# A four-stage conv/Mamba network on one core: tile waits by bytes instead of by pool, and a first Mamba front of its own

## The chip, the cores and the metric

The kernel runs on one core of a Trainium2 chip, as one program from the input image to the output. The metric is the device time of one execution in microseconds (us), smaller being better. Three runs of the kernel before took 8290.22, 8294.99 and 8299.15 us; the median, 8294.99, is what a changed kernel is compared with.

A core has five engines that run side by side and each take their instructions in order: TensorE (PE) multiplies matrices, VectorE (DVE) and GpSimd (POOL) do elementwise work, ScalarE (ACT) applies functions, and SyncE (SP) issues transfers. Semaphores order them.

## The reference

The input x has 4 images of 96 channels and 64 x 64 pixels in float32. Four blocks follow one another, each with weights of its own:

1. A Mamba fusion block. Each image is a sequence of 4096 tokens with 96 features. Two Mamba layers are added to it in turn, and then their output is joined with a pooled vector of the image by a 1x1 product, normalised by a batch norm over all images, and added to the block's input. One Mamba layer is, cut to what matters:

```python
h = layernorm(seq) * ln_g + ln_b
xs, z = split(h @ in_w)                       # 192 channels each
xc = silu(causal_conv(xs, 4 taps) + conv_b)
dt, Bm, Cm = split(xc @ xproj_w)              # 6, 16 and 16 rows
delta = softplus(dt @ dt_w + dt_b)
dA = exp(delta[..., None] * A)
dBx = delta[..., None] * Bm[:, :, None, :] * xc[..., None]
state = scan(dA, dBx)                         # s_t = dA_t * s_(t-1) + dBx_t
y = (einsum('blds,bls->bld', state, Cm) + Dp * xc) * silu(z)
seq = seq + y @ out_w
```

2. An SSD block: a Mamba-2 layer run over each image in four scan directions, with an RMS norm ahead, 3 heads of 64 channels and a state of 128.
3. A second Mamba fusion block.
4. A ConvNeXt block: depthwise convolution, layer norm, two products with a GELU between them, a scale, and the residual.

The batch norm between blocks 1 and 2, and between 3 and 4, needs the mean and the variance of the whole fused output. Nothing of block 2 that depends on normalised values can begin before the last pixel of block 1 is there.

## The kernel before, in words

`program` calls, twice, `mamba_fusion` and then a block: `ssd` the first time and `convnext` the second. A Mamba stage writes its fused output without the batch norm into a DRAM tensor `raw`, and returns two vectors per channel, `bn` (L712 to L724); the block behind it loads `raw` and applies them (for SSD the steps `affine` L871 and `residual` L872, for ConvNeXt L1577 and L1579).

**A Mamba stage.** It takes 32 steps: 4 images, 2 layers, 4 pieces of 1024 tokens. A step is a front and 24 groups.

- The front (`mamba_front`) works on a piece X: `pc` centers it by a matmul (L166), `sq` squares, `pv` averages (L175), `rs` is the inverse root, `h` the normalised input (L182, L185). `pu` multiplies h with the convolution already folded into the input weights (L196, 8 matmuls for each of three channel groups j), `x` is its Silu, `pz`/`z` the gate, `pd`/`dbl` the small projection (L227, L231), which goes to DRAM as `rows` (L235). From there B and C are loaded, spread over partitions, as `bc` (L277). `pt`/`delta` is the softplus (L246), `du` delta times x on POOL (L258); both are stored as `dd` and `dg` (L263).
- A group (class `Scan`) takes 8 of the 192 channels with their 16 states, on 128 partitions, over the two halves of the piece (512 tokens each). It loads `da` from `dd`, and in 7 of 24 groups `du` from `dg` as well (L332, two transfers of 256 KB each, five groups ahead, into 9 buffers). ACT makes the exponential with `w_a` in place (L110). `bs` is du times B: in 17 groups PE spreads it with the selector `seldu` (L346) and DVE multiplies it with bc (L369), in 7 POOL makes the product (L354). DVE scans (L374), POOL multiplies the states `hs` with C into `hc` (L381), PE sums over states with `selsum` (L395), and once per j DVE closes y (L412).
- Behind the last j, PE projects (L425), ACT adds into X (L617), and for layer 2 the piece goes out to `raw` (L632) with sums for the batch norm (L629).

The order of all this is written out by hand in `Scan.run`: for every group it issues the stages with their lags, and inside the groups it advances the front of the next step by a table `PACE` (age of the front in groups, number of parts). Each engine is held to the order in which the code issues. The first front has no groups to run beside: before, it is the same generator `mamba_front`, exhausted before `Scan.run` begins.

**Around the stages** the order isn't written by hand. The set-up of a stage (weights, constants made by memsets and selects, first loads) stands in the code behind the stage ahead, and the scheduler of the tile framework may put an instruction earlier on its engine when what it depends on allows that. That is where the pools come in. All tiles come from tile pools, two to four for each stage (`m1`, `mwork`, `mstate`; `s1`, `swork`; `c1`, `cwork`; and one in PSUM each). Pools of a stage are closed at its end and their bytes given to the next stage's pools. By the framework's default a tile of a new pool waits for every user of the pool that had its bytes before:

```python
one = ctx.enter_context(tc.tile_pool(name="m1", bufs=1))
work = ctx.enter_context(tc.tile_pool(name="mwork", bufs=1))
psum = ctx.enter_context(tc.tile_pool(name="mps", bufs=2, space=PSUM))
```

The tiles at the boundaries that later sections name are, in SSD: `ones`, `tri`, `mask` (a triangle of ones), `inw` and `conv` (the input weights, and convolution weights multiplied by them, L805, from which `sconv` is spread), `xn` (the normed input with its border, memset at L785), the pieces `X` of `raw`, `pk` (packed input for the matmuls) and `dr`. In Mamba: `one`, `seldu`, `selsum`, the weights `w_...`. In ConvNeXt: `band` (four padded images, memset at L1563, filled at L1579), `quad`, `taps`, `diag` (the depthwise weights as diagonals, L1597 to L1606), `shifted` and `strips` (copies of the band for PE and DVE, L1623, L1625), `dw` and `acc` (the convolution on PE and on DVE, L1661, L1676).

Of the kernel before, what the change touches and what calls it, by code (L numbers as in the profile page):

```python
# [18 lines left out]
F32 = mybir.dt.float32  # L19
# [106 lines left out]
def rsqrt(act, out, in_, eps):  # L126

    act.exp_ln(out, in_, AF.Ln, bias=eps)
    act.exp_ln(out, out, AF.Exp, scale=-0.5)


# [15 lines left out]
def mamba_front(tc, k, x_in, pools, wt, parts, c, h, made):  # L147
# [148 lines left out]

PACE = {
    0: 2, 1: 1, 2: 1, 3: 1, 4: 1, 6: 1, 7: 2, 8: 1, 9: 2, 10: 1, 11: 2, 12: 1, 13: 2, 15: 1, 16: 1,  # L300
    17: 2, 18: 1, 19: 1, 20: 1, 21: 1, 22: 1, 23: 1, 28: 1, 29: 1, 30: 1, 31: 1,
}
# [5 lines left out]
class Scan:  # L308
# [125 lines left out]
    def run(self, steps, wts, front, first, later):  # L434
# [18 lines left out]
        for n in range(-LEAD, total + 26):  # L453
# [28 lines left out]
            for began, parts in fronts:  # L482
                for _ in range(PACE.get(n - began, 0)):
                    next(parts, None)
# [76 lines left out]
def mamba_fusion(ctx: ExitStack, tc, k, src, dst, w):  # L561

    nc = tc.nc
    one = ctx.enter_context(tc.tile_pool(name="m1", bufs=1))

# [14 lines left out]
    fetch(2)  # L580
    work = ctx.enter_context(tc.tile_pool(name="mwork", bufs=1))
    state = ctx.enter_context(tc.tile_pool(name="mstate", bufs=3))
    psum = ctx.enter_context(tc.tile_pool(name="mps", bufs=2, space=PSUM))
    dram = ctx.enter_context(tc.tile_pool(name="mdram", bufs=3, space=DRAM))
# [17 lines left out]
    for b in range(2):  # L602
# [3 lines left out]
        )  # L606
    for q in range(NQU):
        pq = psum.tile([P, T], F32, tag="mm", name="pq")[:, :QUART]
        nc.tensor.transpose(pq, sel["du"][:QUART, 0, q], k.ident[:QUART, :QUART])
        nc.vector.tensor_copy(sel["sum"][:, q], pq)  # L610

# [34 lines left out]
    def front(n, made):  # L646
        b, sub, c = steps[n]
        pooled = None if sub else parts[:, b]
        return mamba_front(
            tc, k, chunks[b * NS + c], (work, psum, dram), wts[sub], pooled, c, h, made  # L650
        )

    for _ in range(4):
        fetch()
# [4 lines left out]
    gpw = one.tile([C, C], F32, name="gpw")  # L659
    made = {}  # L660
    for _ in front(0, made):
        pass

    def other_weights():

        yield from mamba_weights(nc, k.act, k.ident, one, w, 1, wts[1])
        nc.sync.dma_start(gpw, w["gp_wT"])
        nc.sync.dma_start(fus, w["fus_wT"].rearrange("(q c) o -> c q o", q=2))
        nc.sync.dma_start(vec, w["vecs"])
        yield  # L670
# [14 lines left out]
    def pooled_rows(b):  # L685
# [13 lines left out]
    each = 3 * HALFP // HEIGHT  # L699
    later = [(each, other_weights()), (2 * each - 2, folded())] + [  # L700
        ((2 * b * NS + NS) * each - 2, pooled_rows(b)) for b in range(B)
# [44 lines left out]
class Ssd:  # L746
# [7 lines left out]
    def __init__(self, ctx, tc, k, src, dst, w):  # L754
        nc = self.nc = tc.nc
        self.k, self.w, self.dst = k, w, dst
        self.raw, self.res, self.bn, self.src = src
        one = self.one = ctx.enter_context(tc.tile_pool(name="s1", bufs=1))
        self.work = ctx.enter_context(tc.tile_pool(name="swork", bufs=2))
        self.psum = ctx.enter_context(tc.tile_pool(name="sps", bufs=2, space=PSUM))  # L760
        self.dram = ctx.enter_context(tc.tile_pool(name="sdram", bufs=2, space=DRAM))
# [32 lines left out]
    def weights_of(self, w):  # L794
# [4 lines left out]

        conv = self.work.tile([P, 3 * BLK], F32, tag="pk", name="conv")  # L800
        conv = conv[:C, : 4 * DI].rearrange("c (k n) -> c k n", k=4)
        nc.sync.dma_start(conv, w["conv_wT"][:, :DI].partition_broadcast(C))
# [742 lines left out]
def convnext(ctx: ExitStack, tc, k, src, out, w):  # L1545

    raw, before, (bn_scale, bn_shift), src = src
    nc = tc.nc
    one = ctx.enter_context(tc.tile_pool(name="c1", bufs=1))
    work = ctx.enter_context(tc.tile_pool(name="cwork", bufs=2))  # L1550
    psum = ctx.enter_context(tc.tile_pool(name="cps", bufs=2, space=PSUM))

# [136 lines left out]
    def bank(tag, bufs):  # L1689
        return psum.tile([P, T], F32, tag=tag, name=tag, bufs=bufs)  # L1690
# [193 lines left out]
```

## Time and profile before

| | us |
|---|---|
| Median of three runs (8290.22 to 8299.15) | 8294.99 |
| The profiled execution: own time | 8294.08 |
| The profiled execution: span | 8292.4 |
| Mamba 0 (to its bn vector) | 0 to 2703 |
| SSD (to its last x store) | 2703 to 4997 |
| Mamba 1 | 4997 to 7707 |
| ConvNeXt | 7707 to 8292 |
| First scan of Mamba 0 / of Mamba 1 | 66.8 / 5060.1 |
| DVE, POOL, PE, ACT busy, of the span | 91%, 82%, 87%, 63% |

The span is the time between the first and the last instruction that the profiler recorded; the own time is what the same execution took by the device's clock, 1.7 us more. A stage has no mark of its own in the trace. Its borders are read from instructions: the end of `bn`, the last store of x. The busy shares are averages over four stages with different limits, so they say little on what a stage waits for. Windows cut at the borders say more.

In a line of the timeline the columns are start, duration, engine (SPq is SyncE's queue of transfers), line of the code, operation, output and inputs, shapes and count, and in square brackets the idle time of the engine before it and what ended that. A row of the waits is: engine, what waited, what it waited for, total us, times, and the longest.

### The profile page before, as it was taken

Reading aid. Unit: us, or ns where it says so; the run is one execution under the profiler, and the core shown is the slowest. Engines: PE = TensorE matmul, PEld = TensorE weight load, DVE = VectorE, ACT = ScalarE, POOL = GpSimd, SP = SyncE. Lnnn points to the kernel's source line nnn. Section 1 sums busy time; section 2 is a strip of 40 time slices with the busy share of each in tenths; the row PEclk is TensorE's granted clock in tenths of the full one; section 3 lists DMA queues with packets and bytes.
Section 4 is the critical chain, followed back from the end, with each engine's and each line's share of the span. In section 5 each row is a group of like instructions: output and inputs, shape, how many; then the busy total and the mean of one; then the engine's idle time right before and its main releaser. Section 6 shows DMA issues by size and latency. Waiting matters only on the chain. (4 is left out here: it accounts for less than half of the span.)

```text
span 8292.4 us, 111766 instructions
## 1 busy us (share of the span) xinstructions
PE 7184.2 (87%) x33944; PEld 3173.3 (38%) x33944; DVE 7523.9 (91%) x8897; ACT 5227.7 (63%) x9510; POOL 6788.3 (82%) x4589
## 2 busy tenths in 40 slices
PE   7888888888887899999999997888888888887688
PEld 1222222222221687898888882222222222221122
DVE  6999999999998799998999996999999999999786
ACT  5666666666664677777777765666566666655255
POOL 6999999999998587887878886999999999999211
PEclk9999989999998899999999998999999999988799
DMA  7989889999997433433333326999898999888553
GB/s 195 240 234 250 232 238 242 238 238 246 246 233 198 116 94 105 113 100 115 96 109 109 93 77 179 240 239 248 230 244 239 245 236 247 236 231 223 120 128 75
DMA packets 819139, 1558.50 MB, mean 188 GB/s; under 512 B 117613, under 2 KB 123529, under 8 KB 815466
## 3 DMA queue, kind: packets, MB, share of 16 engines
q1 hardware_dynamic: 815466, 1546.23, 71.0%
q8 instruction: 272, 4.46, 0.2%
q10 hardware_dynamic: 3072, 5.11, 0.2%
q14 instruction: 329, 2.70, 0.1%
HBM read 1256.10 MB, written 148.50 MB: 169 GB/s over the span
## 5 line engine op out<-in xcount | busy, mean ns | idle before, releaser
L381 POOL TENSOR_TENSOR hc<-hs,bc 128x1024 f32<-128x1024 f32 x1536 | 3603.4, 2361 | 404.1 <-DVE hs L374 314.1
L374 DVE TENSOR_TENSOR_SCAN hs<-da,carry,bs 128x1024 f32<-128x1024 f32 x816 | 1914.9, 2347 | 121.6 <-issue 47.0
L346 PE MATMUL bs<-du,seldu 64*128 64x512 f32 x4352 | 1420.8, 696 | 652.7 <-DVE hs L374 647.4
L369 DVE TENSOR_TENSOR bs<-bs,bc 128x1024 f32<-128x1024 f32 x1088 | 1319.7, 1213 | 113.4 <-PE bs L346 91.4
L110 ACT ACTIVATE da<-da,w_a 128x1024 f32<-128x1024 f32 x1088 | 1230.7, 1140 | 5.3 <-DMA da<-dd 3.1
L354 POOL TENSOR_TENSOR du<-du,bc 128x1024 f32<-128x1024 f32 x448 | 1060.0, 2366 | 26.5 <-DMA da<-dd 13.7
L346 PEld LDWEIGHTS bs<-du,seldu 64*128 64x128 f32 x4352 | 396.8, 199 | 1629.0 <-issue 1160.0
L395 PE MATMUL py<-hc,selsum 128*32 128x512 f32 x6144 | 838.5, 616 | 33.3 <-DVE y L412 20.6
L110 ACT ACTIVATE bs<-da,w_a 128x1024 f32<-128x1024 f32 x448 | 500.2, 1116 | 534.2 <-DVE hs L374 244.4
L196 PE MATMUL pu<-h,w_conv 96*64 96x512 f32 (+1 forms) x3072 | 824.1, 657 | 7.8 <-ACT h L185 7.2
L374 DVE TENSOR_TENSOR_SCAN hs<-bs,carry,du 128x1024 f32<-128x1024 f32 x336 | 781.4, 2326 | 0.0
L374 DVE TENSOR_TENSOR_SCAN hs<-da,bs 128x1024 f32<-128x1024 f32 x272 | 622.1, 2287 | 40.3 <-issue 14.1
L1129 DVE SCALAR_TENSOR_TENSOR bc<-front,taps,bc 128x384 f32<-128x384 f32 (+1 forms) x1152 | 648.8, 564 | 0.5
L1094 PE MATMUL front<-sconv,pk 128*128 128x192 f32 x3072 | 596.3, 331 | 16.9 <-ACT z L1146 11.8
L1254 POOL TENSOR_TENSOR xs<-x,coef 128x576 f32<-128x576 f32 x512 | 590.8, 1154 | 16.4 <-DVE y L1332 14.8
L1323 POOL TENSOR_TENSOR y<-y,xs 128x192 f32<-128x192 f32 x496 | 294.3, 593 | 363.0 <-DVE y L1316 358.7
L1338 ACT ACTIVATE y<-yz 128x192 f32<-128x192 f32 x512 | 183.9, 359 | 548.2 <-DVE yz L1333 475.7
L1223 POOL TENSOR_TENSOR seg<-dr,mask 128x384 f32<-128x384 f32 x512 | 512.3, 1001 | 9.7 <-DMA dr<-rows 9.7
L1094 PEld LDWEIGHTS front<-sconv,pk 128*128 128x128 f32 x3072 | 493.8, 192 | 28.0 <-ACT z L1146 18.6
L110 ACT ACTIVATE seg<-seg,ndac 128x128 f32<-128x128 f32 x1536 | 499.2, 388 | 4.5 <-POOL prev L1282 1.3
L1676 DVE SCALAR_TENSOR_TENSOR acc<-strips,kern,acc 128x512 f32<-128x512 f32 x504 | 425.4, 846 | 51.0 <-ACT acc L1666 18.3
L115 ACT ACT_TABLE_LOAD x352 | 451.6, 1283 | 8.6 <-ACT dtrow L938 3.0
(225 smaller groups left out, 12778.7 us busy)
## 6 DMA issues: line engine op xcount, KB each, us to landing
da<-dd SPq DMA_DIRECT2D x3072, 256.0 KB
du<-dg SPq DMA_DIRECT2D x896, 256.0 KB
dr<-rows SPq DMA_DIRECT2D x256, 384.0 KB
bc<-rows SPq DMA_DIRECT2D x256, 256.0 KB
dd<-delta SPq DMA_DIRECT2D x192, 256.0 KB
dg<-du SPq DMA_DIRECT2D x192, 256.0 KB
pk<-xn SPq DMA_DIRECT2D x128, 384.0 KB
pk<-xn SPq DMA_DIRECT2D x128, 256.0 KB
```

The lines of the kernel that those rows point to most:

```text
L110: self.last = self.scalar.activation(out, in_, func, **kw)
L196: nc.tensor.matmul(pu[HALFP * i : HALFP * (i + 1)], lhsT=wt["conv"][:kk, tap, D0[j] : D0[j] + HALFP], rhs=h[:kk, ds(i * T + tap, T)], star ...
L346: nc.tensor.matmul(g["bs"][:, i], lhsT=self.sel["du"][rows, g["half"], g["q"]], rhs=g["made"]["du"][rows, g["j"]], start=True, stop=True,)
L354: self.tc.nc.gpsimd.tensor_tensor(g["du"], g["du"], self.b_or_c(g, 0), ALU.mult)
L369: nc.vector.tensor_tensor(dbx, dbx, self.b_or_c(g, 0), ALU.mult)
L374: nc.vector.tensor_tensor_scan(out, da, dbx, init, ALU.mult, ALU.add)
L381: nc.gpsimd.tensor_tensor(g["hc"], hs, self.b_or_c(g, 1), ALU.mult)
L395: nc.tensor.matmul(py[ds(HALFP * i + QUART * x["half"], QUART)], lhsT=self.sel["sum"][:, q], rhs=x["hc"][:, i], start=(q == 0), stop=(q == ...
L1094: nc.tensor.matmul(p, lhsT=held["pk"][:, i, ds(order[m] * Q, Q)], rhs=self.conv[:, i], start=(i == 0), stop=(i == 2),)
L1129: nc.vector.scalar_tensor_tensor(out, shifts[tap], self.taps[:, q, tap : tap + 1], out, ALU.mult, ALU.add)
L1223: self.nc.gpsimd.tensor_tensor(seg, g["pair"]["dr"][:, ds(g["c"] % 2 * NH, NH)], self.mask[:, g["r"]].to_broadcast([P, NH, Q]), ALU.add,)
L1254: self.nc.gpsimd.tensor_tensor(xs, x.to_broadcast([P, 3, NH, HD]), coef.to_broadcast([P, 3, NH, HD]), ALU.mult)
```

## The change

The change has three parts.

1. The pools of a stage are taken apart. A class `Laid` opens many small pools with `reuse_waits="tile"`, each for one or a few tags, in a written order; with it a tile waits only for users of the bytes that it takes over. The order lays the tiles of a stage by when the stage ahead is done with those bytes. The PSUM pools are treated likewise, one for each tag. `work`, `state` and `one` become names for the same set of pools.
2. The first front of a Mamba stage is a routine of its own, `first_front`. In it the convolution of group j goes from PSUM through Silu straight into x, and the gates likewise, between them; h is scaled on DVE, not ACT; dbl is evicted by DVE; the two averages `pv` have a PSUM bank each; the copies of X that sum for the pooled vector come at its end. It yields once delta is made, and the rest (the remaining stores, products and bc loads) is issued inside the first groups through `later`, from group -5 on. The transposes that make `selsum` come behind it (`sum_rows`). The front of the second step follows a table `LATE`, which starts at an age of 5 groups and has the same entries as `PACE` from 16 on.
3. SSD's convolution weights get a tile of their own, `convw`, where they were in a slot of `pk`.

The diff, cut to its core:

```diff
+class Laid:
+    def __init__(self, ctx, tc, name, order, **space):
+        self.pools = {}
+        for i, tags in enumerate(order):
+            pool = ctx.enter_context(
+                tc.tile_pool(name=f"{name}{i}", bufs=1, reuse_waits="tile", **space)
+            )
+            self.pools.update(dict.fromkeys(tags.split(), pool))
+
+    def by(self, bufs):
+        return LaidPool(self.pools, bufs)
...
+def first_front(tc, k, x_in, pools, wt, parts, h, made):
...
+    for n, tag in enumerate(("po", "py")):
+        pc = bank("mm", 2)[:C]
+        nc.tensor.matmul(pc, lhsT=k.center, rhs=xs[n], start=True, stop=True)
+        sq = work.tile([P, T], F32, tag="ua", name="sq", bufs=3)[:C]
+        nc.scalar.activation(sq, pc, AF.Square)
+        pv = bank(tag, 1)[:C]
+        nc.tensor.matmul(pv, lhsT=k.mean, rhs=sq, start=True, stop=True)
+        rs = work.tile([P, T], F32, name="rs", bufs=2)[:C]
+        rsqrt(k.act, rs, pv, k.eps[:C])
+        nc.vector.tensor_tensor(into[n], pc, rs, ALU.mult)
+        nc.vector.tensor_scalar(
+            into[n], into[n], wt["ln"][:, 0:1], wt["ln"][:, 1:2], ALU.mult, ALU.add
+        )
...
+    for j in range(3):
+        pu = bank("mm", 2)
...
+        k.act.other(x[:, j], pu, AF.Silu, back=False)
+        if j == 1:
+            gate(0)
+    pd = bank("po", 1)
+    for j in range(3):
+        if j == 2:
+            gate(1)
+        rows_of(pd, j)
+    gate(2)
+    dbl = work.tile([P, T], F32, name="dbl")
+    nc.vector.tensor_scalar_add(dbl, pd, wt["one"])
+    rows = dram.tile([P, T], F32, name="rows")
+    nc.sync.dma_start(rows, dbl)
...
+        k.act.other(deltas[j], pt, AF.Softplus, back=(j == 2))
+        if j == 0:
+            store("dd", 0, deltas[0])
+            spread(0)
+            sized(0)
+    for n in range(2):
+        unused = work.tile([P, T], F32, tag="ua", name="copy", bufs=3)[:C]
+        nc.scalar.activation(unused, xs[n], AF.Copy, accum_out=parts[:, n : n + 1])
+    yield
+    store("dg", 0, du[:, 0])
+    sized(1)
+    yield
...
+LATE = {
+    5: 2, 6: 1, 7: 1, 8: 2, 9: 2, 10: 2, 11: 2, 12: 2, 13: 2, 14: 2, 15: 1, 16: 1,
+    17: 2, 18: 1, 19: 1, 20: 1, 21: 1, 22: 1, 23: 1, 28: 1, 29: 1, 30: 1, 31: 1,
+}
...
-                for _ in range(PACE.get(n - began, 0)):
+                for _ in range((LATE if began < 0 else PACE).get(n - began, 0)):
...
-    one = ctx.enter_context(tc.tile_pool(name="m1", bufs=1))
+    laid = Laid(ctx, tc, "m", (
+        "h w_ln0 w_in0 w_conv0 w_xproj0 w_dt0 w_dd0 w_d0 w_a0 w_out0 one7", "dbl", "delta", "rs",
+        "seldu", "du", "x", "ua", "bc", "X", "z", "hs", "da", "y", "hc", "*",
+    ))
+    one = work = state = laid.by(1)
...
-    psum = ctx.enter_context(tc.tile_pool(name="mps", bufs=2, space=PSUM))
+    psum = Laid(ctx, tc, "mps", ("mm", "po", "py", "bs"), space=PSUM).by(2)
...
+    ahead = first_front(tc, k, chunks[0], (work, psum, dram), wts[0], parts[:, 0], h, made)
+    next(ahead)
+    sum_rows()
...
-    for _ in front(0, made):
-        pass
...
-    later = [(each, other_weights()), (2 * each - 2, folded())] + [
+    later = [(-5, ahead), (each, other_weights()), (2 * each - 2, folded())] + [
...
+        laid = Laid(ctx, tc, "s", (
+            "ones tri norm epsn inw convw sconv xbias bcbias taps a ad", "xn0 xn1", "pk", "nx nr", "nsq",
+            "dtx ua row", "z", "X", "mask opw gn", "*",
+        ))
+        one, self.work = laid.by(1), laid.by(2)
...
+        self.psum = Laid(ctx, tc, "sps", ("front", "halves", "y", "out"), space=PSUM).by(2)
...
-        conv = self.work.tile([P, 3 * BLK], F32, tag="pk", name="conv")
-        conv = conv[:C, : 4 * DI].rearrange("c (k n) -> c k n", k=4)
+        conv = one.tile([C, 4, DI], F32, name="convw")
...
+    laid = Laid(ctx, tc, "c", (
+        "taps kern conv_b quad diag c_vecs c_w1 c_b1 c_w2 shift", "turned", "band0", "band1",
+        "band2", "band3", "raw before", "*",
+    ))
+    one, work = laid.by(1), laid.by(2)
+    psum = Laid(ctx, tc, "cps", ("hid", "dw", "ln", "out"), space=PSUM).by(2)
```

## The prediction

> **What bounds the kernel now.** I read the windows table first, cut where the stages change: Mamba 0 runs to 2703 us, the SSD block to 4997, Mamba 1 to 7707, the ConvNeXt block to the end. Its columns after the window are busy us (instructions) of PE, PEld, DVE, ACT and POOL, then granted TensorE clock, DMA share, GB/s.
>
> ```profile
> 0.00:67.00 67.00, 43.78 (x120) 12.15 (x122) 8.03 (x20) 34.57 (x48) 11.92 (x16) 0.92 0.49 131
> 67.00:148.00 81.00, 65.00 (x260) 15.43 (x256) 77.72 (x46) 52.16 (x81) 73.23 (x33) 0.89 0.96 243
> 148.00:2600.00 2452.00, 2101.11 (x8341) 512.30 (x8341) 2329.56 (x1395) 1549.88 (x2305) 2276.79 (x1022) 0.94 0.92 240
> 2600.00:2677.00 77.00, 54.53 (x182) 13.47 (x182) 71.84 (x43) 25.25 (x31) 66.84 (x30) 0.75 0.63 160
> 2677.00:2703.00 26.00, 17.67 (x24) 4.16 (x24) 4.34 (x12) 4.08 (x12) 3.27 (x2) 0.55 0.07 22
> 2703.00:2797.00 94.00, 68.72 (x232) 38.54 (x233) 48.64 (x106) 47.35 (x89) 20.10 (x19) 0.71 0.47 130
> 4955.00:4992.00 37.00, 26.42 (x181) 21.77 (x179) 24.42 (x61) 14.64 (x58) 28.25 (x38) 1.00 0.00 1
> 4992.00:5060.00 68.00, 42.69 (x118) 15.57 (x120) 7.39 (x16) 33.18 (x47) 11.40 (x10) 0.72 0.56 153
> 7600.00:7681.00 81.00, 54.62 (x192) 13.32 (x190) 75.85 (x45) 28.35 (x34) 70.69 (x31) 0.79 0.62 160
> 7707.00:7741.00 34.00, 9.31 (x72) 2.75 (x76) 14.09 (x19) 4.26 (x6) 9.28 (x4) 0.59 0.65 147
> ```
>
> Inside a Mamba stage DVE is the bound (2330 of 2452 us, 95%), with POOL at 93% and DMA at 92% close behind. Between stages nobody is: DVE works 8 of the first 67 us, 4 of 26 at 2677, 7 of 68 at 4992, 14 of 34 at 7707. Then DVE's waits say what it waits for at the beginning (0 to 67 us) and around 5000:
>
> ```profile
> DVE h L182 <- ACT rs L110: 43.2, 4, 34.0
> DVE h L182 <- ACT rs L110: 36.7, 4, 26.5
> DVE h L594 <- DMA x<-X: 7.8, 1, 7.8
> ```
>
> The timeline shows the last two as a chain, and the same behind the other boundaries:
>
> ```profile
> 4990.88 0.69 DVE L1388 TENSOR_TENSOR X<-X,out 96x256 f32<-96x256 f32 x1 [1.21 <-PE out L1371]
> 4991.60 3.51 SPq L1395 DMA_DIRECT2D x<-X  x4
> 4998.87 0.10 POOL L587 MEMSET one<- 128x1 f32 x1 [12.44 <-DMA x<-X]
> 5037.01 0.34 SPq L235 DMA_DIRECT2D rows<-dbl  x1
> 5046.81 2.45 SPq L332 DMA_DIRECT2D da<-dd  x4
> 5060.13 2.29 DVE L374 TENSOR_TENSOR_SCAN hs<-da,bs 128x1024 f32<-128x1024 f32 x1
> ...
> 2703.30 3.51 POOL L785 MEMSET xn<- 1x4102 f32 x1 [21.74 <-DVE bn L724]
> 2719.53 0.95 DVE L805 TENSOR_TENSOR conv<-conv,inw 96x768 f32<-96x768 f32 x1 [7.18 <-DMA inw<-in_L_in]
> ...
> 7707.40 9.28 POOL L1563 MEMSET band<- 96x2692 f32 x4 [21.74 <-DVE bn L724]
> 7709.79 6.94 DVE L1604 COPY quad<-ident 32x32 f32<-32x32 f32 x3
> ```
>
> The reader is to see that a memset, which needs nothing but its own bytes, waits 12 or 22 us for the last user of the whole former pool; behind it hang all weights, and from there 61 us (4999 to 5060) pass to the first scan.
>
> **The change, by parts.** The instruction counts barely move: over the program DVE gets 6 instructions more (four h multiplications and two dbl evictions that ACT had), ACT 16 fewer, 6 table loads (1.28 each) among them, PE, POOL and the DMA count are unchanged. Inside the stages the waits on the scans, bs products and loads are the same but for a handful. So the 2452-us bodies are costed at nothing, and the sum is made of four boundaries.
>
> *Start (0 to 67).* The new front squares straight away, starts the convolution matmuls with the first h, applies Silu from PSUM group by group (six of about 0.6 us, beside PE), and puts dbl on DVE. Before: h ready at 17.8 and 23.9, convolution to 35.3, then copies, a table load 1.28 and Silu 1.48 over 1536 columns, rows stored at 43.5, delta at 48.1, da loads at 53.8, first scan 66.8. Walking the new order with those durations: h at 16.5, first third of the convolution at about 23 (w_a still lands at 21.6), rows at 35, dd at 38, da loads at 40, first scan about 47, 20 us earlier. But the next 81 us run at a DMA share of 0.96 and 243 GB/s: a 256-KB load costs 256/243 = 1.08 us and a group needs two (four in 7 of 24 groups). In the old order part of that queue was filled while DVE idled; a scan that starts 20 us earlier starts with fewer groups in hand. I give back 7: **13** (8 to 19). The second front is paced to begin later but stores its rows at the same place (group 16), so nothing there: PE, 65 of 81 us busy, has to hide it, and each group that it slips costs 81/24 = 3.4.
>
> *Mamba 0 to SSD (2677 to 2797).* Weights, tri, mask, residual and first X loads go ahead of the batch-norm vector bn (2702.9). What must follow bn are the affine steps. Before, the first ran at 2706.3, the third only at 2720.0, since its loads sat in SP behind others that waited; after that a chunk takes 3.75 us, and the last xn ends at 2745.2. With three X chunks ready at bn and ACT busy about 2.9 us per chunk the eight take 25 to 30 us: last xn near 2730, 15 earlier. Price in the tail of Mamba 0: DVE gets the conv product (0.95, at L805 it waited 7.2 for its load), ones 0.17, memsets 0.6; POOL 1.1 for tri and 3.5 for one xn memset, ahead of the last two hc; SP gets about 1 MB (4 us at 240 GB/s) in a stretch with a DMA share of 0.63. I charge 3: **12** (5 to 17).
>
> *SSD to Mamba 1 (4955 to 5060).* All weights, X loads and selectors go ahead of the four x stores, and the new front interleaves with the last projections: h at 4996.5 where it was 5012.5, rows about 5015.5 (5037.0), da loads 5020.4 (5046.8), first scan 5028 (5060.1), 32 earlier; the same warm-up gives back 6. Price: the SSD tail is paced by POOL (28.3 of 37 us), which gets seldu's memset 0.95, two selects of 2.05 and two of 0.23, 5.5 in all; DVE gets 3 us, ACT the exponential of w_a, which is queued ahead of SSD work and needs all 16 w_a loads (11.6 us of issue). These follow the last dr load on SP, well ahead, in a stretch with DMA at 0.00. Charge 4: **22** (12 to 30).
>
> *Mamba 1 to ConvNeXt (7600 to 7741).* Band memsets, taps, quad and diag go into Mamba 1's tail; the raw loads stay behind the last raw stores. The band additions, which stood behind the quad copies (7716.8 to 7722.3), follow the affines at about 7709 to 7714; first acc at 7734 where it was 7741.1: 7 gained. Against it stand 4 quad and 7 taps copies on a DVE that is 94% busy (75.85 of 81). A taps copy alone takes 0.16, a quad copy beside a POOL memset 2.3 (above: three in 6.94), ending each time with the memset. The Trainium skill, "SBUF — State Buffer", section Who interferes with whom, says why this speaks against the change: a copy that DVE runs over both port pairs and a GpSimd instruction exclude each other for the whole instruction, and whichever begins first blocks the other. By the rule each copy, and diag (0.96, two SBUF inputs), may wait for the rest of an hc (2.36, POOL 87% busy): 12 x 1.18 x 0.87 = 12 us on average, 25 at most. The nearest row of the trace for the other end: the scalar product of w_a at 195.8, in a stretch where POOL is 93% busy, took 0.15, since it stood right behind a scan and hc started after it; 12 such cost 2 to 3. In the new order half of the copies stand behind a scan, half behind a bs product with an hc under way: 8. **-1** (-12 to +8).
>
> Sum 13 + 12 + 22 - 1 = 46. The profiled execution took 8294.1 (its span is 8292.4), 0.9 under the median 8295.0; 8294.1 - 46 = 8248, as a median **8249**.
>
> **The rivals.**
> *A, the warm-up takes it back.* DMA (0.96) and POOL (73 of 81) are as full as DVE just behind both Mamba starts. For it: if the old first scans lived on loads queued during the idle time, 12 to 15 us of each start come back instead of 6 or 7, and the tails cost half as much again as my charges of 3, 4 and 8: 46 - 14 - 7 = 25 gained, 8270. Against: the 24th group comes 80 us after the first scan both in the start and at 5060, hardly slower than the 79 to 85 of a later step.
> *B, the waits stay.* A tile's bytes may have late users (bn's chain, the last hc), or the queue order holds the set-up back; then only the new front gains, perhaps 12: 8283, same. Against: the program's order shows the set-up in front of bn and of the x stores.
> *C, slower: an instruction of the next stage stands at the head of an in-order queue and waits for a transfer.* Place: DVE's conv product ahead of some twenty scans of Mamba 0, behind its own load, which stands in SP behind da loads that wait for buffers that DVE frees; and w_a's exponential in the SSD tail. A wait stops DVE, then the da loads behind the sconv copies on SP. Price: 7.2 us as DVE waited at L805, 11.6 for w_a, and after each a refilling of the 5-group lead, 17 us (5 x 3.4): 24 and 29; with 25 for the copies 78. The four parts gain 61 before my charges (46 + 3 + 4 + 8): 17 slower, 8312. It decides from 61 us of such stalls on. Against: both loads are issued groups ahead.
>
> **How the numbers follow.** Forecast 0.62, A 0.20, B 0.06, C 0.12. About 0.2% (17 us) is what a measurement of this kernel can tell from no change (its runs lie between 8290 and 8299). Faster 0.62 + 0.20 = 0.82, same 0.06, slower 0.12. The four parts' bounds, not all at one end, give 8222 to 8272; the range reaches into B: 8220 to 8283, which leaves out C and the far ends.
>
> **What would show it.** Right: first scan at 45 to 50 us and the 24th group's at 130 to 136 (now 146.0); last xn 25 to 30 us behind bn; first scan of Mamba 1 within 40 us of the last SSD addition (now 69); no POOL memset with 12 or 22 us of idle time before it; quad copies of mixed length, 0.1 to 2.4, among the last scans. Wrong: Mamba bodies whose length changes by over 5 us, a DVE or ACT wait of over 5 us on a weight load before bn or before the last x store, or a first scan early and a 24th group no earlier than now.

## The result, and the profile after

The changed kernel takes 8267.86 us (median of 5 runs, 8253.47 to 8274.96) against 8294.99 us of the kernel before: a ratio of 0.9964 with a 95% interval of 0.9949 to 0.9978. It is faster by 27 us where 46 were forecast. The profiled execution has a span of 8266.1 us. A second set of five runs gave 8272.77 us against 8296.29.

The windows of the profile after, cut at the events themselves where those shown of before are cut near them (columns as there):

```profile
0.00:47.40 47.40, 33.82 (x106) 10.57 (x106) 8.46 (x21) 19.19 (x33) 9.60 (x15) 0.96 0.40 103
47.40:136.50 89.10, 69.99 (x262) 17.65 (x264) 77.65 (x47) 56.09 (x86) 73.67 (x34) 0.83 0.95 259
2589.20:2676.10 86.90, 54.94 (x182) 13.62 (x182) 78.52 (x50) 27.57 (x34) 73.19 (x32) 0.76 0.68 176
2676.10:2701.10 25.00, 18.54 (x24) 4.20 (x24) 4.21 (x19) 4.08 (x12) 7.09 (x3) 0.52 0.35 104
4925.40:4983.00 57.60, 46.80 (x251) 39.59 (x251) 38.36 (x95) 26.68 (x89) 46.10 (x59) 0.76 0.22 54
4983.00:5017.00 34.00, 26.85 (x101) 7.95 (x99) 4.85 (x10) 15.40 (x27) 3.71 (x3) 0.95 0.41 126
5017.00:5106.50 89.50, 70.27 (x262) 17.69 (x264) 77.66 (x47) 56.14 (x86) 73.94 (x34) 0.83 0.95 257
7488.30:7663.00 174.70, 123.67 (x438) 29.97 (x440) 163.63 (x101) 75.47 (x109) 150.18 (x66) 0.80 0.75 191
7689.10:7713.70 24.60, 10.28 (x76) 3.10 (x80) 3.01 (x7) 4.27 (x6) 0.53 (x1) 0.61 0.83 184
```

The idle stretches are shorter, as the change says: 47.4 us to the first scan, 34.0 from SSD's last addition to Mamba 1's first scan, 24.6 from bn to ConvNeXt's first acc. But the rows beside them are longer. For the same work the kernel before shows, in the same view:

```profile
66.80:146.00 79.20, 63.45 (x252) 15.27 (x248) 75.95 (x45) 50.16 (x78) 71.23 (x33) 0.89 0.96 240
4943.50:4991.60 48.10, 35.91 (x244) 29.65 (x243) 34.46 (x88) 24.24 (x83) 39.75 (x53) 1.00 0.06 18
7518.50:7683.20 164.70, 120.66 (x443) 29.12 (x440) 152.26 (x87) 75.49 (x109) 147.10 (x65) 0.84 0.76 201
```

These are the first step of Mamba 0 (79.2, after 89.1), SSD's last ten additions (48.1, after 57.6) and the last two steps of Mamba 1 (164.7, after 174.7). The first step of each Mamba stage went from 79.3 and 79.9 us, first scan to first scan, to 89.2 and 89.5. In Mamba 0's, VectorE stands idle for 11.4 us where it stood for 3.2; the other 1.7 us are more work of VectorE, most of it the second front's h, which stood ahead of the first scan before. In the timeline after, the chain at 4983 reads:

```profile
4982.25 0.72 DVE L1547 TENSOR_TENSOR X<-X,out 96x256 f32<-96x256 f32 x1 [1.90 <-PE out L1530]
4983.00 3.28 SPq L1554 DMA_DIRECT2D x<-X  x4
5005.29 0.34 SPq L391 DMA_DIRECT2D rows<-dbl  x1
5011.25 1.16 SPq L483 DMA_DIRECT2D da<-dd  x2
5017.03 2.29 DVE L525 TENSOR_TENSOR_SCAN hs<-da,bs 128x1024 f32<-128x1024 f32 x1 [1.96 <-ACT da L110]
```

From the last addition's end to rows it is 22 us (before 45), to the da loads 28 (before 55). No memset stands behind the stores any more.

### The profile page after: what moved, and what is told of

Same layout as the page of the kernel before. It is cut to its first block, busy times and chain, and to the rows that moved or that the text cites. A ratio compares the mean times of both kernels' runs of the same rounds, so it can differ in the third digit from the quotient of the medians.

```text
span 8266.1 us, 111696 instructions
## 1 busy us (share of the span) xinstructions
PE 7193.8 (87%) x33944; PEld 3180.7 (38%) x33944; DVE 7532.2 (91%) x8903; ACT 5208.4 (63%) x9494; POOL 6790.8 (82%) x4589
## 5 line engine op out<-in xcount | busy, mean ns | idle before, releaser
L505 POOL TENSOR_TENSOR du<-du,bc 128x1024 f32<-128x1024 f32 x448 | 1060.9, 2368 | 24.4 <-DMA du<-dg 14.4
L546 PE MATMUL py<-hc,selsum 128*32 128x512 f32 x6144 | 840.7, 617 | 37.9 <-DVE y L563 24.5
L220 PE MATMUL pu<-h,w_conv 96*64 96x512 f32 (+1 forms) x2976 | 792.2, 654 | 11.3 <-ACT h L209 11.3
```

The lines of the kernel that those rows point to most:

```text
L220: nc.tensor.matmul(pu[HALFP * i : HALFP * (i + 1)], lhsT=wt["conv"][:kk, tap, D0[j] : D0[j] + HALFP], rhs=h[:kk, ds(i * T + tap, T)], star ...
L505: self.tc.nc.gpsimd.tensor_tensor(g["du"], g["du"], self.b_or_c(g, 0), ALU.mult)
L546: nc.tensor.matmul(py[ds(HALFP * i + QUART * x["half"], QUART)], lhsT=self.sel["sum"][:, q], rhs=x["hc"][:, i], start=(q == 0), stop=(q == ...
```

## The experiments

The places in eight of the profiles, in us, read from scans, additions and bn in each trace: a step or a tail goes from the start of its first instruction to the end of its last (the first step of Mamba 1 to the start of the second), and the stretches between them are what is left. "24th group" is the scan that the prediction calls so, the first of the second step. The medians come from four sets of runs, each with runs of before beside it.

| | before | after | front_alone | pools_alone | mended | pace | less_dma | best |
|---|---|---|---|---|---|---|---|---|
| 0 to the 24th group's scan | 146.0 | 136.5 | 135.0 | 151.2 | 137.8 | 134.9 | 133.4 | 138.4 |
| last step of Mamba 0, scans | 80.9 | 86.9 | 80.8 | 86.8 | 87.4 | 86.8 | 87.5 | 80.8 |
| last scan to last xn of image 0 | 66.1 | 52.8 | 66.2 | 52.8 | 49.2 | 52.8 | 52.8 | 53.0 |
| SSD's last ten additions | 48.1 | 57.5 | 50.2 | 56.9 | 49.6 | 58.7 | 54.8 | 49.4 |
| last addition to first scan | 68.6 | 34.1 | 50.6 | 54.3 | 34.9 | 40.0 | 34.7 | 40.8 |
| first step of Mamba 1 | 79.9 | 89.5 | 86.9 | 79.8 | 86.5 | 79.8 | 86.0 | 83.7 |
| last two steps of Mamba 1, to bn | 188.6 | 200.8 | 187.9 | 197.2 | 188.4 | 199.7 | 201.8 | 193.2 |
| bn to first acc | 34.0 | 24.6 | 33.8 | 24.5 | 27.0 | 24.9 | 25.3 | 27.6 |
| sum, less that of before | 0 | -29.5 | -20.8 | -8.7 | -51.4 | -34.6 | -35.9 | -45.3 |
| median time of the runs | 8295 to 8299 | 8267.9, 8272.8 | 8278.7 | 8268.9, 8269.2 | 8259.2 | 8259.0 | 8253.6 | 8248.9 |

**The front alone** (new `first_front` and `LATE`, pools of before):

```diff
-    laid = Laid(ctx, tc, "m", (...))
-    one = work = state = laid.by(1)
+    one = ctx.enter_context(tc.tile_pool(name="m1", bufs=1))
+    work = ctx.enter_context(tc.tile_pool(name="mwork", bufs=1))
+    state = ctx.enter_context(tc.tile_pool(name="mstate", bufs=3))
...
```

> The new first front with its pacing, in the old pools with their old waits. Theory (the gains are those of separate places, and each start gives back what its warm-up takes): first scan at about 47 us and about 5040 (20 earlier each), the 24th group's scan 9 to 10 us earlier than before in each Mamba stage, the set-up of SSD and ConvNeXt as before, no conv product waiting on VectorE at 2630; in all 18 to 20 us faster than before, 8275. Rival (the front brings something only where the pools let it start early): 9 us, all of it at the first start, 8286.

Measured: 8278.72 us, ratio 0.9976 (0.9966 to 0.9986). First scan at 47.2; in each stage the 24th group gains 10 to 11 us (135.0 for 146.0, and 50.6 + 86.9 for 68.6 + 79.9). The tails are as before. The theory holds; the routine brings 11 us per start, not 20, since the first step takes 88 and 87 us where it took 79 and 80.

**The pools alone** (the opposite half: `Laid` and `convw`, front of before), run twice:

> The laid pools with tile waits and the convw tile, with the old first front. Theory (separate places): the first 24 groups as before; SSD's last first-image xn 14 us sooner after bn; the conv product again stops VectorE for about 6 us in Mamba 0's tail and the quad copies cost about 7 us in Mamba 1's; SSD's tail about 9 us longer; Mamba 1's first scan about 12 us sooner after the last SSD addition. Sum 5 to 12 us faster than before, 8285. Rival (set-up in the tails costs as much as it brings): within 4 us of before, or slower.

> The kernel of pools_alone once more, profiled and timed again. By the places at the boundaries its profile was 9 us shorter than the one before, but its median was 28 us lower; the other 20 us lie in the long Mamba and SSD bodies (groups 96 to 720 of Mamba 1 took 2109 us, before 2126). Theory (the bodies scatter by some 10 us from execution to execution and the pools alone bring about 9): body of Mamba 1 2113 to 2125 in this profile, median 8280 to 8290. Rival (the laid pools make the bodies shorter): body below 2112 again, median about 8269.

Measured: 8268.92 and 8269.17 us, ratios 0.9963 (0.9949 to 0.9978) and 0.9969 (0.9956 to 0.9981). Most places are as expected: set-up of SSD 13 us shorter, conv product waiting 5.1 us, SSD's tail 9 longer, Mamba 1's first scan 14 sooner. One is not: the 24th group of Mamba 0, expected as before, comes 5 us later (151.2 for 146.0) in both profiles, since the first scan comes at 71.0 and 70.9 for 66.8; no run looks into why. The places sum to 9 us, and the median gained 27 to 28. The expectation of 8285 was wrong, in both runs. In the profiles 9 to 13 us of the rest lie where the change has nothing: groups 24 to 720 of Mamba 1 took 2365 and 2369 us with these pools, 2378 in both profiles of before. In the changed kernel, with the same pools, they took 2382 and 2368, so the pools aren't shown to be the cause. Why the same instructions run shorter there was not found out, and with it the medians of the halves (18 and 28 us) don't add up to that of the whole, while their places (20.8 and 8.7) do.

**The kernel before and the changed kernel, profiled again:**

> The kernel before, profiled a second time, for the scatter of what no part of the change touches. Theory (scatter): boundaries the same to within 1 us as in the first profile; the three bodies (2115, 2126 and 2127 us) each within 12 us of the first. Rival (before's bodies are long in every execution): Mamba 1's body again 2124 or more.

> The changed kernel once more, profiled and timed beside the others. Theory (its gain is what the boundaries show, 29 us): first scan 19 us earlier, 24th group 9 to 10 us earlier, conv product waiting 5 to 7 us, SSD's last ten additions 57 us, one quad copy after another beside POOL; median 8262 to 8272. Rival (the gain also lies in the bodies): the three bodies together 15 us or more shorter than before's 6368.

Before took 8287.42 us in this one run. Its boundaries repeat within 1.5 us but for SSD's tail (50.6 for 48.1), and so do its bodies (2112, 2126, 2125; first 2115, 2126, 2127). So the rival of the first expectation came true: Mamba 1's body is not scattered in before, it is 2126 both times. The changed kernel repeats at the boundaries (57.5 for SSD's tail, 174.7 for the last two steps of Mamba 1, the conv product waiting 6.2 us), but for the first steps: 87.1 and 87.2 us where the first profile has 89.2 and 89.5. Its median, 8272.77, is a little above the expected range. Its three bodies sum to 6365 and 6363, before's to 6368 and 6363: in these profiles its gain is at the boundaries.

**The default waits between the small pools:**

```diff
-                tc.tile_pool(name=f"{name}{i}", bufs=1, reuse_waits="tile", **space)
+                tc.tile_pool(name=f"{name}{i}", bufs=1, **space)
```

> The changed kernel with the default waits between pools (a tile waits for all users of the small pools whose bytes its pool takes), layout and front kept. Theory (what counts is that a tile waits only for its own bytes): the set-up of SSD starts behind bn again in large part, and that of Mamba 1 behind the last x store: total 10 to 18 us slower than the changed kernel, 8280. Rival (the order of the small pools does it, the waits by tile add nothing): within 5 us of the changed kernel, 8268, with the same instructions ahead of bn.

Measured: 8266.86 us (0.9963, 0.9949 to 0.9978), the changed kernel's time, with the conv product ahead of bn (it waits 6.0 us at 2638) and 34.1 us from last addition to first scan. The rival holds: taking the large pools apart, in this order, does it. Waits by tile add nothing that these runs can see. What the title and the first part of the change call waits by bytes is, in its effect, the taking apart of the pools. Whether the written order or the bare splitting does it, and how much of it hangs on `convw` (the tile that lets the conv product go ahead), no run separates.

**Mended tails:**

```diff
-        nc.vector.tensor_copy(quad[part, 0], k.ident[part, part])
+        nc.scalar.copy(quad[part, 0], k.ident[part, part])
...
-        nc.sync.dma_start(conv, w["conv_wT"][:, :DI].partition_broadcast(C))
+        nc.scalar.dma_start(conv, w["conv_wT"][:, :DI].partition_broadcast(C))
...
-        nc.gpsimd.memset(x, 0.0)
+        if n < 2:
+            nc.gpsimd.memset(x, 0.0)
+        else:
+            nc.gpsimd.tensor_scalar(x, bn_shift.to_broadcast(x.shape), 0.0, 0.0, ALU.mult, ALU.mult)
...
+        nc.sync.dma_start(
+            sel["du"], k.saved[:, 1:].rearrange("p (b q m) -> p b q m", b=2, q=NQU)
+        )
```

> The changed kernel with four costs of the tails taken away: the conv weights' load is issued by ScalarE instead of behind the da loads, so that the conv product has its data (6.3 us of VectorE idle before); the four quad copies on ScalarE (7 us); the zeroing of bands 2 and 3 made to follow bn (2.1 us); the selector of Mamba 1 loaded from a copy that Mamba 0 saved, not built on POOL (5 us of POOL in SSD's tail). Theory (these costs are what the prediction mis-sized in the tails, each in full): last Mamba 0 step 81 us again, SSD's last ten additions 4 to 5 us quicker, Mamba 1's last two steps 8 to 10 us quicker: 16 to 21 us faster than the changed kernel, 8248. Rival (VectorE's waits only move to the next late thing, a da load or POOL): at most 8 us, 8260.

Measured: 8259.19 us (0.9954, 0.9942 to 0.9966), 9 below the changed kernel where 16 to 21 were expected (22 by the places; in this profile SSD's body was 2133 us for 2125). Two of the four costs went as the theory says, or better. SSD's tail, in the same windows as above, is back:

```profile
4936.80:4986.40 49.60, 39.58 (x251) 33.67 (x251) 38.15 (x95) 26.67 (x89) 40.77 (x53) 0.93 0.30 72
```

POOL has 40.8 us of work for 46.1, and PE's granted clock is 0.93 for 0.76. With the quad copies on ScalarE the last two steps of Mamba 1 take 164.4 us for 174.7, and with the bands zeroed behind bn the stretch from their end to bn takes 23.9 for 26.1, so 188.4 for 200.8 in all. But the bands' zeroing only moved: from bn to the first acc it is 27.0 us for 24.6. The fourth failed: the conv product waited 6.7 us as before, now for inw, whose load I had left on SP.

**inw on ScalarE's queue too:**

```diff
-        nc.sync.dma_start(self.inw, w["in"])
+        nc.scalar.dma_start(self.inw, w["in"])
```

> The mended kernel with inw's load issued by ScalarE as well; in the mended kernel the conv product still waited, for inw. Theory (VectorE stood still for 6 us only because the load was issued just ahead): wait for the load under 1 us, the last Mamba 0 step 81 us instead of 87, total 5 to 6 us below the mended kernel, 8253. Rival (the load isn't served faster than 7 us beside the da loads and VectorE only waits at another place): step still 86 or 87.

Measured: 8254.42 us (0.9948, 0.9936 to 0.9960). The last step is 80.1 us, as the theory says, but the step before is 91.3 for 83.7. The trace names it (the tile's instructions, and what they waited for):

```profile
L979 DVE TENSOR_TENSOR convw<-convw,inw x1: 954/954/954, 2593.6 to 2593.6; 96x768 f32<-96x768 f32 x1
its engine sat idle before it (us, times) until:
  DMA convw<-in_L_conv_wT: 9.8, 1
```

The scheduler put the product earlier along with its load, and the load, issued at 2576.4 among da loads, landed at about 2593. The trace gives 2592.8 for inw, issued at 2574.1. The rival holds: the wait moved, and grew.

**A warm PE** (mended_inw, and two matmuls without use per group at the end of each Mamba stage):

```diff
+            for _ in range(2 if total - 20 <= n < total + 3 else 0):
+                warm = self.psum.tile([P, T], F32, tag="mm", name="warm")
+                self.tc.nc.tensor.matmul(
+                    warm, lhsT=self.k.ident, rhs=made[-1]["x"][:, 0], start=True, stop=True
+                )
```

> The same as mended_inw, with two matmuls whose result nobody reads put on PE per group over the last 20 groups of each Mamba stage and three behind. Last scan to bn took 25 or 26 us with a granted clock of 0.52 and 19.5 with 0.70. Theory (a PE that waits much is granted half the clock, and the last projections then run at 1.06 us each instead of 0.53): granted clock in that stretch 0.9 or more, last scan to bn 17 to 19 us at both boundaries, total 10 to 14 us below mended_inw. Rival (the clock does not follow the filler matmuls, or they delay the bs products by as much): within 4 us of mended_inw or slower.

Measured: 8257.12 us (0.9950, 0.9937 to 0.9962). The clock follows, the time doesn't. From last scan to bn of Mamba 0, with the clock at 1.00, and in pools_alone without the filler:

```profile
2706.60:2727.20 20.60, 15.85 (x47) 4.80 (x45) 9.09 (x24) 4.08 (x12) 9.45 (x3) 1.00 0.49 143
```

```profile
2684.00:2703.50 19.50, 13.09 (x24) 2.99 (x24) 4.16 (x19) 4.08 (x12) 6.97 (x3) 0.71 0.44 132
```

The rival holds, in its second half. Last scan to bn is 20.6 and 22.5 us where mended_inw has 18.7 and 25.2 (granted clock 1.00 and 0.82 for 0.79 and 0.50), and the last xn follows 27.7 us later for 33.5; but the last step takes 90.1 and 87.7 us for 80.1 and 81.6. In Mamba 0's, VectorE waits 6.8 us for bs products from PE where it waited 1.0, and 2.8 for a set-up tile of SSD. (A last projection of Mamba 0 takes 1.06 us in the changed kernel, as the expectation says, and 0.59 here, not 0.53.) The stretch to bn alone misleads, too: in the kernels with laid pools it is 19 us with 33.5 to the last xn behind it, or 25 with 27.8, and the sum is 52.3 to 53.1 in all but mended (49.2) and warm (48.3).

**The pacing, and lighter first loads.** These two look into the first step:

```diff
-                for _ in range((LATE if began < 0 else PACE).get(n - began, 0)):
+                for _ in range(PACE.get(n - began, 0)):
```

> The changed kernel with the second front of each stage paced by the old table (it starts with the loop, not 5 groups later). Theory (the first 24 groups run 10 us long because the first loads come late and ScalarE and TensorE pass that on: h of the second front stands behind an exponential that waits for a da load, the conv matmuls behind h, a bs product behind those): with h and the conv matmuls ahead of the first group, the 4.5-us wait for PE in group 3 goes, the first scan comes 3 to 8 us later, and the 24th group's scan within 3 us of the changed kernel's; total the same, 8268. Rival (the pacing is what costs the start): the 24th group's scan 5 us or more earlier in both stages, total 8258.

```diff
-                last=(q == NQU - 1 and p == 1), dma=(p == 1 and (q % 2 == 0 or (j, q) == (2, 1))),
+                last=(q == NQU - 1 and p == 1),
+                dma=(p == 1 and (q % 2 == 0 or (j, q) == (2, 1))) and (n, j) != (0, 0),
```

> The changed kernel with the two groups of j = 0 in every step 0 (the very first step of the program only for the pair: image 0, layer 1, piece 0 of each Mamba stage) that load du made from PE and VectorE instead: 1 MB less to load in the first 12 groups, two POOL products less, two VectorE products of 1.21 us more. Theory (DMA bandwidth and POOL's late product set the warm-up): the waits of VectorE for POOL's du (2.5 and 3.3 us) and about half of the wait for PE vanish; the 24th group's scan 2 to 5 us earlier after the first scan, in each stage. Rival (the order on ScalarE and PE sets it): VectorE's 2.4 us of more work appear in full, 24th group 0 to 3 us later.

Measured: pace 8258.99 us (0.9950, 0.9936 to 0.9965), less_dma 8253.61 (0.9948, 0.9936 to 0.9959). With pace the first scan is at 54.2, 7 later, and the first step takes 80.7 and 79.8: the 24th group comes 1.6 us earlier in Mamba 0 and 3.8 in Mamba 1 (0.4 and 2.5 against the second profile of the changed kernel). By the places that is the theory with an edge for the old table: what the new pacing wins ahead of the first scan it pays behind it. The total is the one that the rival forecast, 8258, but from 8238.86 to 8273.44 its six runs cover the theory's 8268 too, so the total decides nothing. For less_dma, VectorE's waits in the first groups of the changed kernel and of this one are

```profile
DVE bs L520 <- PE bs L497: 4.8, 2, 4.5
DVE hs L525 <- POOL du L505: 2.5, 1, 2.5
DVE hs L525 <- ACT da L110: 2.1, 1, 2.1
```

```profile
DVE hs L525 <- ACT da L110: 1.3, 1, 1.3
DVE h L206 <- ACT rs L110: 1.2, 1, 1.2
```

Two groups whose du need not be loaded take away the waits for POOL and for PE, and the 24th group comes 3 us earlier in both stages (1.8 and 1.5 against the second profile of the changed kernel), with 2.4 us more of VectorE's work. That is the theory's side, but the edit takes POOL's two products out along with the loads, so the loads alone aren't shown to set the warm-up, and the first step still takes 84.3 and 86.0 us where before has 79.3 and 79.9. The total moved by more than the places (36 us by places, 46 by medians).

**All together:**

```diff
-        nc.vector.tensor_tensor(conv, conv, xs[:, None].to_broadcast([C, 4, DI]), ALU.mult)
+        unit = one.tile([C, 1], F32, name="unit")
+        nc.vector.tensor_scalar(unit, self.bn[1], 0.0, 1.0, ALU.mult, ALU.add)
+        nc.vector.scalar_tensor_tensor(
+            conv, conv, unit, xs[:, None].to_broadcast([C, 4, DI]), ALU.mult, ALU.mult
+        )
...
```

> Everything that the runs point to in one kernel: the changed kernel, with the quad copies on ScalarE, bands 2 and 3 zeroed behind bn, Mamba 1's selector loaded from a copy, the sign of a turned on ScalarE, the two first du loads replaced as in less_dma, the old pacing of the second front, and the conv product made to follow bn (multiplied by a one that is computed from bn). Theory (each cost was in one place): no VectorE wait for a conv load, last Mamba 0 step 81 us, 24th group's scan 132 us, SSD tail 50; 8 to 12 us below mended_inw: 8244. Rival (the conv product behind bn delays the first SSD chunk by as much, or the old pacing and the lighter loads don't add): 8250 to 8256.

Measured: 8248.92 us (8232.46 to 8252.00), ratio to before 0.9937 (0.9924 to 0.9951). It beats both kernels: in the same set the changed kernel took 8272.77. The conv product that must follow bn costs nothing visible (53.0 us to the last xn, 52.8 before it was moved), and the step it had stopped is 80.8 us:

```profile
2593.90:2674.70 80.80, 55.47 (x182) 13.47 (x182) 75.71 (x48) 27.83 (x35) 71.73 (x31) 0.75 0.68 176
```

It lands 5 us above its expectation. The pacing and the lighter loads don't add: the 24th group is at 138.4, where 132 was expected and either edit alone gave 133 to 135. Why is open, and the place itself scatters: in kernels whose start is that of the changed one it is at 135.2 to 137.9 (after_again 135.2, warm 135.7, mended_inw 137.9).

## Why the prediction was right, and where it was off

The direction and the place of the gain were right, and the time lies in the range, but 46 us were forecast and 27 came. The places of the profile give 29.5, so the sum can be checked term by term. That the total is so near rival A's 8270 is luck: A gave back 12 to 15 us at each start and let the tails cost half as much again as the charges, 22 in all; the starts gave back under 10 and the tails cost 27.6 where 15 were charged. Of the mechanism, the waits on whole large pools are shown to be what held the set-up back (pools_alone), and `reuse_waits="tile"` is shown to be needless (pool_waits). `LATE`, the new pacing, brought nothing that the places show (pace).

*Start: 13 forecast, 9.5 measured.* First scan 47.3 (forecast about 47). The give-back was mis-sized: 7 was taken, 9.9 it is. In Mamba 1 likewise, 6 taken and 9.6 measured. The second profile has 7.8 and 7.3, so the miss is 1 to 4 us. Nor does the give-back end at the 24th group: the second step, which the prediction's "79 to 85 of a later step" leaves out, takes 88.2 and 87.9 us before, and 88.2 and 94.9 after (87.2 and 87.9 in the second profile). The timeline of groups 1 to 3 shows how late loads spread:

```profile
51.36 2.34 POOL L505 TENSOR_TENSOR du<-du,bc 128x1024 f32<-128x1024 f32 x1 [9.46 <-DMA du<-dg]
53.73 2.29 DVE L525 TENSOR_TENSOR_SCAN hs<-bs,du 128x1024 f32<-128x1024 f32 x1 [2.54 <-POOL du L505]
55.71 1.15 ACT L110 ACTIVATE da<-da,w_a 128x1024 f32<-128x1024 f32 x1 [4.23 <-DMA da<-dd]
56.77 1.51 ACT L209 ACTIVATE h<-h,w_ln 96x512 f32<-96x512 f32 x2
57.62 4.38 PE L220 MATMUL pu<-h,w_conv 96*64 96x512 f32 x8 [5.78 <-ACT h L209]
61.93 2.08 PE L497 MATMUL bs<-du,seldu 64*128 64x512 f32 x4
64.06 1.23 DVE L520 TENSOR_TENSOR bs<-bs,bc 128x1024 f32<-128x1024 f32 x1 [4.54 <-PE bs L497]
```

A da load is late, ScalarE stands at its exponential, h of the second front is behind it in ScalarE's queue, the conv matmuls behind h on PE, and the bs product behind those. The prediction counted bytes for VectorE and not this detour. pace takes the detour away, less_dma takes loads and POOL products away, and each gets the 24th group only 0 to 4 us earlier; so the detour is where the time goes, and what sets it is only in part shown.

*Mamba 0 to SSD: 12 forecast.* The set-up is as forecast (from the last scan to the last xn 13.3 us less, which holds the 15 gained behind bn and about 1 lost ahead of it). The charge of 3 for the tail was wrong; the last step is 6.0 longer:

```profile
2628.62 0.50 SPq L961 DMA_DIRECT2D convw<-in_L_conv_wT  x1
2636.21 0.95 DVE L964 TENSOR_TENSOR convw<-convw,inw 96x768 f32<-96x768 f32 x1 [6.34 <-DMA convw<-in_L_conv_wT]
```

This is rival C's mechanism at the place that it named and near the price that it named (7.2 there, 6.34 here), but once, and without the refilling of 17 us behind it. The step that failed is "both loads are issued groups ahead": inw's load is issued at 2612.67, 17 us before VectorE arrives, but conv's only 1.3 us before. It is held in SP behind da loads, and the last of these waits, by the profile, not for a buffer that VectorE frees, as rival C has it, but for the landing of inw (SP's waits, 2600 to 2640):

```profile
SPq L483 <- DMA inw<-in_L_in: 4.8, 1, 4.8
```

So a slow set-up load, 15 us from issue to landing, held up the next one. ScalarE's w_a exponential, the second place of rival C, did not wait. A wait of over 5 us on a weight load before bn stands among the prediction's own signs of being wrong; it came, and cost 6 us, not the forecast. Of the signs of being right two fall short: the 24th group is at 136.5 for 130 to 136 (135.2 in the second profile), and one band memset still waits 17.2 us (last line of the block on ConvNeXt below). The others came.

*SSD to Mamba 1: 22 forecast, 15.5 measured* (34.5 from the first scan, less 9.6 in the first step, less 9.4 in SSD's tail). The first scan came 2.5 us better than forecast. The tail's charge of 4 was mis-sized: POOL got the 5.5 us that the prediction lists, in full since POOL paces the tail, and PE's granted clock fell from 1.00 to 0.76; the last additions waited 1.9 to 2.1 us for PE where they waited 1.2. The cost of 9.4 is 7 against the second profile of before, whose tail takes 50.6. mended, which takes POOL's work away and leaves the rest, gets both back; so POOL's work is shown as the cause of the tail's length, the clock's part in it is not separated.

*Mamba 1 to ConvNeXt: -1 forecast, -2.8 measured.* The gain behind bn was 9.4 (forecast 7), the price 12.2 (forecast 8):

```profile
7544.56 2.10 DVE L1766 COPY quad<-ident 32x32 f32<-32x32 f32 x1
7551.18 4.87 DVE L1766 COPY quad<-ident 32x32 f32<-32x32 f32 x3
7551.35 2.36 POOL L505 TENSOR_TENSOR du<-du,bc 128x1024 f32<-128x1024 f32 x1
7553.67 2.34 POOL L532 TENSOR_TENSOR hc<-hs,bc 128x1024 f32<-128x1024 f32 x1
7620.08 2.36 POOL L532 TENSOR_TENSOR hc<-hs,bc 128x1024 f32<-128x1024 f32 x1
7620.70 0.25 DVE L1759 COPY taps<-kern 32x12 f32<-32x12 f32 x2
7684.95 2.40 DVE L870 TENSOR_SCALAR means<-means,mv 96x32 f32<-96x32 f32 x1
7684.98 4.65 POOL L1725 MEMSET band<- 96x2692 f32 x2 [17.21 <-ACT sqs L784]
```

The rule weighed there (the Trainium skill, "SBUF — State Buffer", section Who interferes with whom) is seen again: all four quad copies end 0.04 us behind the end of a POOL instruction. Three took 2.1 to 2.3 us; one, the first of the three, began 0.2 us before such an end and took 0.25. The diag product, 0.96 alone, took 2.03. The term that was mis-sized is "each copy": the seven taps copies took 0.13 to 0.17 each though all began while a POOL instruction was under way, as the pair at 7620 did, and five ended a microsecond or more before it. They were not held at all, so whether they stand behind a scan or behind a bs product has no part in it. Why a 32x12 copy passes and a 32x32 copy doesn't, no run here shows. What the prediction did not see is the last pair of lines: a band memset hoisted to where its bytes come free runs beside the bn chain, and a VectorE instruction of that chain takes 2.40 us where before it took 0.24:

```profile
7705.13 0.24 DVE L714 TENSOR_SCALAR means<-means,mv 96x32 f32<-96x32 f32 x1 [0.71 <-ACT sqs L629]
```

That is on the path that sets the end, with no cover at all. Quad copies 7.0, diag 2.0, taps 1.0 and this 2.2 come to the 12.2.

By the terms: 46 forecast, less 3.5 at the start, less 4.7 from Mamba 0 to SSD (13.3 - 6.0 = 7.3 for 12), less 6.5 and less 1.8, is the 29.5 of the places. Between these and the medians (27, and 24 in the second set) lie 2 to 6 us, inside the interval. That they agree so well is no proof of the sum: for pools_alone the same sum missed the median by 19 us, for mended by 14. Three readings of the prediction itself were off, without weight for the total: 17.8 is where VectorE begins the first h (it is ready at 20.6), 256-KB loads at 243 GB/s take 1.08 us only by 262 kB (256/243 is 1.05), and the bounds that give 8222 are all four at their good end (19 + 17 + 30 + 8 = 74).

## What to carry to other kernels

When set-up work is let into the tail of a busy stage, price it at the tail's bound: what goes on the engine that paces the tail costs its full length, a copy on VectorE beside a busy POOL can cost up to one POOL instruction (here the 32x32 copies did and the 32x12 copies did not), and an instruction that needs a load costs what the load still needs when its engine gets there. Check, for each hoisted instruction with a load, what stands ahead of that load in its queue. A stage that starts earlier starts with fewer loads in hand; here two fifths to a half of what the first scan of Mamba 0 won was given back within the first step (8.5 of 19.6 us in front_alone, 9.9 of 19.4 in the changed kernel), so count on that much until the first step's waits have been read.

## What had not been expected of the hardware

- Lengths of a Mamba step, first scan to first scan, gather on a few values: 78.7, 80.2, 80.5, 81.6, 83.0 and 84.6 us come again and again in all kernels, 78.7 most of all, in sequences that differ from kernel to kernel and sometimes between two executions of one (the 31 differences in Mamba 1 of before repeat to 0.3 us in its second profile, those in Mamba 0 don't). A body that no edit touches so differs by some 10 us between kernels and executions; that a small shift at its start picks the sequence is a guess that no run tests. That is the scatter that a sum over places has to live with.
- A load of 295 KB beside the da loads was awaited until 7.6 us after its issue at 2628.6 us, and in mended_inw, on ScalarE's queue, until 17 us after its issue at 2576.4, where the queue's instruction itself took 4.4 us.
- Filler matmuls raised the granted PE clock from last scan to bn from 0.79 to 1.00 in Mamba 0 and from 0.50 to 0.82 in Mamba 1 (warm against mended_inw), and the stretch went from 18.7 to 20.6 us and from 25.2 to 22.5: a faster clock alone did not make it reliably shorter.
